# Two transformer layers on one core: closing steps cut into pieces among products, the token table turned later, opening loads reordered

## The chip, the core and the metric

The kernel runs on one core of a Trainium2 chip, all in fp32. The metric is the device time of one execution in microseconds. The core has a matrix engine (TensorE, PE in the profile), a vector engine (VectorE, DVE), an activation engine (ScalarE, ACT), a general engine (GpSimd, POOL) and a queue engine that issues transfers (SyncE, SP); ACT and POOL can issue transfers too. Each engine takes its instructions in order, and engines wait for each other by semaphores.

## The reference, cut to what matters

The input is x, 8 sequences of 256 tokens of width 512. Two layers follow each other; each normalizes x and adds an attention part and a feed-forward part to it.

```python
# layer 0, attention: 32 heads of 128, with decays along the sequence
qkv = silu(xn @ qkv_w.T)
attn = blockwise(q, k, v, decays)            # (q k^T * decay) v, causal
xf = attn * rsqrt(mean(attn * attn over all 4096) + EPS)
a0 = (sigmoid(xn @ gate_w.T) * norm_w * xf) @ out_w.T
# layer 0, feed-forward: 16 experts, 2 chosen per token, and a shared one
scores = softmax(xn @ router_w + router_b) + router_bias   # best 2 of 4 groups, best 2 in them
y = sum over chosen e: score[e] * ((silu(xn @ w1[e] + b1[e]) * (xn @ w2[e] + b2[e])) @ w3[e] + b3[e])
x = x + a0 + y + shared(xn)
# layer 1, attention: one head of 128, softmax; feed-forward: 64 pieces of rank 16
G = softmax of the 16 best of xn @ Wr.T, zero elsewhere    # [tokens, 64]
f1 = (h * G) @ B * 2.0, with h = xn @ A.T
x = x + softmax_attention(xn) + f1
```

## The kernel before

**Staging.** The 2048 tokens are four chunks `i` of 512 (four tiles `t` of 128). The opening (to about 148 us) normalizes the chunks, routes the tokens, runs the shared expert (L355) and transposes the rows; PE is warmed by `WARM` transposes of the identity (L205). Then come 32 units `(i, g)`, one for each chunk and each of eight groups of four heads, chunk by chunk. A unit's projections q, k, gate, v are made by products of quarters of tokens and weights in the manner of Strassen: seven named products p1 to p7 in the order of `ORDER`, each by an inner scheme of seven more (`go`, L724); in chunk 0 some are plain and use eight. Weights' sums are made in chunk 0 (`w<-w,st` with `st` a staged part of the weights, `w<-w`) and stored for later chunks.

**Slots and pieces.** After each inner product the code calls `slot()`; a unit has 49 slots of about 1.47 us and lasts 72 to 77 us. `later(after, f)` puts the piece `f` on a list, to be run at the slot `now + after` or a later one: a slot runs one piece (two if more than 12 wait), and pieces whose names are on a list count for nothing. Through pieces run the quarter's silu and gate, scores (L846, L847) and attention (L858, L859), the projections through out_w (L935, L955, `acc<-ps_sc,acc`), experts and scatters.

**Experts.** The tokens of one expert tile (47 tiles) are fetched by an expert object: two gathers on POOL's queue (L761 rows, L766 weights), then `turn` transposes them (L775, copied to `xeT` by DVE in L777), `bias` gathers a bias on POOL (L781), `up` multiplies by w1, w2 (L793) and `down` by w3 (L805), after which DVE adds the bias to `ye` and SP stores it. A unit from number 8 on runs two or three experts, 16 slots apart.

**Table.** In chunk 0 `scatter` writes token numbers into a table in DRAM by indirect DMA on POOL; in unit 7 `read_table` loads it into `rows` (47 rows of 8 KB, SP's queue), and `turn_table` 16 slots later copies it to `byno` (DVE), transposes that on PE and copies it to `whose` (DVE), from which experts gather.

**Chunk's end.** `done()` is run about 22 slots into the unit behind a chunk's last one. It sums squares on PE (L1024, eight products of two tiles each), takes the root mean (`rms`), `combine`s the seven parts of `acc` on POOL (chunks 1 and 2 only), `finish`es into `r`, a staged `spare` (DVE, L636), and stores that to `xs_`.

**Second layer.** For each chunk: two `low_rank` calls (`seven`, L1573, with `hg` = product times `spread_g`, gates spread over ranks), then a third `seven` for the second matrix (L1651). A `fill` gives functions to run between the seven products (keys are the product just made): attention of layer 1, and in the third call the next chunk's head (route, q and k, values, softmax, gates). `gather` on POOL fetches the experts' results, `settle` adds them (DVE, L611), `normalize` prepares the next chunk (`spare<-x,mv,rstd`, L256), and `turn_rows` transposes it (L276).

**Order.** PE, DVE and SP are ordered by a planner from the program's order, save for instructions in `tc.keep_in_program_order`. In layer 0, ACT and POOL keep the order of the program.

Of the kernel before, what the change touches and what calls it, by code (L numbers as in the profile page):

```python
# [10 lines left out]
WARM = 16  # L11
SAME = 16
# [57 lines left out]
def block_kernel(  # L70
# [80 lines left out]
    scratch = big("scratch").rearrange("p (h b) n -> p h (b n)", h=4)  # L151
    xs = [work.tile([P, TPC, C], FP, tag="x", name=f"x{i}", bufs=NCH) for i in range(NCH)]
# [3 lines left out]

    rw = once([P, NC, E], "rw")
    nc.sync.dma_start(out=rw, in_=router_w)
    rb = once([P, 1, E], "rb")
# [3 lines left out]
    wsh = staged("wsh")[:, 0 : NC * 2 * SH * P].rearrange("p (c n) -> p c n", c=NC)  # L163
# [3 lines left out]
    bsh_t = once([P, 2, SH], "bsh_t")  # L167
    nc.sync.dma_start(out=bsh_t, in_=b_sh)
    for i in range(1, NCH):
        for t in range(TPC):  # L170
            nc.sync.dma_start(out=xs[i][:, t, :], in_=x_t[i, t])
# [27 lines left out]
    nc.scalar.dma_start(out=wsh, in_=w_sh)  # L199
# [183 lines left out]
    xT, gates, xns = [], [], []  # L383
# [68 lines left out]
    def begin(i):  # L452
        xns.append(work.tile([P, TPC, C], FP, tag="xn", name=f"xn{i}"))
        normalize(xns[i], xs[i], apart=(i == 0), behind=(i == 1))
# [3 lines left out]
    def turn(i):  # L458
        xT.append(work.tile([P, NC, CH], FP, tag="xT", name=f"xT{i}", bufs=3))
        for t in range(TPC):  # L460
            turn_rows(xT[i], xns[i], t, ps_mm())
# [144 lines left out]
    def settle(i, n, x_, y):  # L606

        for t in range(TPC):
# [13 lines left out]
    def combine(i):  # L622

        for o, p in (
            ("p2", "p1"), ("p6", "p1"), ("p7", "p6"), ("p6", "p5"), ("p3", "p6"), ("p4", "p7"), ("p5", "p7"),
        ):
# [3 lines left out]
    def finish(i, r):  # L630

        for b in range(2):
            for t in range(2):
                n = 2 * b + t
                o = r[:, n, :].rearrange("p (h c) -> p h c", h=2)
                nc.vector.scalar_tensor_tensor(  # L636
                    o, acc[i][:, 2 * b : 2 * b + 2, t], all_rms[i][:, n : n + 1], o, ALU.mult, ALU.add
                )

# [9 lines left out]
    with tc.tile_pool(name="attn", bufs=1) as attn, tc.manual_schedule(engines={mybir.EngineType.Activation, mybir.EngineType.Pool}):  # L649
# [94 lines left out]
        def slot():  # L744
# [3 lines left out]
            while pieces and pieces[0][0] <= now[0] and n < (2 if len(pieces) > 12 else 1):  # L748
                f = pieces.pop(0)[2]
                f()  # L750
                n += getattr(f, "func", f).__name__ not in ("silu", "bias", "gate", "read_table", "scatter", "load_sum", "sums1", "sums2", "sums3", "sums4", "settle0", "settle1", "out_sum")
# [135 lines left out]
        class Unit:  # L887
# [129 lines left out]
            def done(self):  # L1017
# [4 lines left out]
                for t in range(TPC):  # L1022
                    for n in range(2):
                        mm(  # L1024
# [736 lines left out]
```

## Time and profile before

| | us |
|---|---|
| median of 3 runs | 2821.71 (2817.76 to 2827.4) |
| profiled execution | 2825.62 |
| its span | 2823.9 |
| PE busy | 2753.2 (97%) |
| DVE, POOL, ACT busy | 1626.7 (58%), 1642.1 (58%), 950.7 (34%) |
| mean granted PE clock | 0.993 |

In what follows a timeline row is: start, length, engine, line, operation, out<-in with sizes, count, and in brackets the idle time ahead of it on its engine with what ended it. A row of waits is: engine and what waited, what it waited for, us in all, times, longest. "Granted clock" is the share of full speed at which PE was allowed to run.

### The profile page before, as it was taken

To read this page: it belongs to the slowest core of one execution; us is meant where nothing else is said; L and a number is where in the kernel's file an instruction comes from. 1 tells how busy PE (TensorE), PEld (TensorE's weight loads), DVE (VectorE), ACT (ScalarE), POOL (GpSimd) and SP (SyncE) were. 2 spreads that over 40 slices of the span, in tenths; PEclk is the share of its full clock that TensorE was granted. 3 is DMA by queue.
4 is the path that set the end of the run, shared out by engine and by line. 5 is a ranking of instruction groups with operands and counts; after the bars stand their busy time and mean duration, and the time that the engine had idled before them with its cause. 6 is when DMAs were issued, how large, how long until landed. Compare 5 with 4: busy or idle time off the path is not lost.

```text
span 2823.9 us, 49588 instructions
## 1 busy us (share of the span) xinstructions
PE 2753.2 (97%) x19641; PEld 2541.2 (90%) x19641; DVE 1626.7 (58%) x2722; ACT 950.7 (34%) x1685; POOL 1642.1 (58%) x1414
## 2 busy tenths in 40 slices
PE   9999999998999999999999999999999999999999
PEld 5699999997999999999899999999999999987877
DVE  7666677776445555555545555555455555656663
ACT  5232222221343333333343333333433333431211
POOL 6477777765556666666655555557555567642220
PEclk9999999999999999999999999999999999999999
DMA  7898888887877777777877777787877788652211
GB/s 288 323 336 328 325 332 332 314 310 300 323 296 292 276 285 271 284 265 294 303 255 269 261 262 272 272 300 279 295 260 263 276 308 311 220 221 68 77 55 62
DMA packets 155063, 752.67 MB, mean 267 GB/s; under 512 B 18721, under 2 KB 25249, under 8 KB 103457
## 3 DMA queue, kind: packets, MB, share of 16 engines
q1 hardware_dynamic: 136528, 677.62, 64.4%
q0 software_dynamic: 17872, 70.32, 7.5%
q8 instruction: 155, 2.54, 0.3%
q10 hardware_dynamic: 432, 1.57, 0.1%
q14 instruction: 76, 0.62, 0.1%
HBM read 605.66 MB, written 142.99 MB: 265 GB/s over the span
## 4 chain that ended last, share of the span: by engine, by line
PE 80%; DVE 7%; DMA 5%; issue 4%; POOL 3%; ACT 0%; SPq 0%; DVEq 0%; POOLq 0%; ACTq 0%
PE ps_a L724 23%; PE ps_e L724 12%; PE ps_sc L935 9%; PE ps_b L724 6%; PE ps_o L858 3%; PE ps_sc L846 3%; PE ps_sc L955 3%; PE ps_sc L793 3%; PE ps_o L859 2%; PE ps_a L1651 2%; PE ps_sc L847 2%; DVE w L100 1%; PE ps_a L1573 1%; PE ps_sc L805 1%; DVE r L100 1%
## 5 line engine op out<-in xcount | busy, mean ns | idle before, releaser
L724 PE MATMUL ps_a<-xt,w 128*128 128x128 f32 x5376 | 751.0, 276 | 13.3 <-DVE r L100 7.1
L724 PEld LDWEIGHTS ps_a<-xt,w 128*128 128x128 f32 x5376 | 685.8, 192 | 39.2 <-issue 12.2
L100 POOL TENSOR_TENSOR c<-c 128x512 f32<-128x512 f32 x240 | 302.7, 1276 | 251.1 <-DVE c L100 242.7
L100 POOL TENSOR_TENSOR c<-c,r 128x512 f32<-128x512 f32 x264 | 347.0, 1335 | 173.1 <-DVE r L100 171.6
L1077 ACT COPY cp<-ps_a 128x512 f32<-128x512 f32 x384 | 224.1, 584 | 607.7 <-PE ps_a L724 586.5
L724 PE MATMUL ps_e<-xt,w 128*128 128x128 f32 x2688 | 375.7, 276 | 8.1 <-DVE c L100 6.7
L724 PEld LDWEIGHTS ps_e<-xt,w 128*128 128x128 f32 x2688 | 342.4, 193 | 16.7 <-DVE c L100 7.3
L100 POOL TENSOR_TENSOR w<-w 128x512 f32<-128x512 f32 x224 | 297.4, 1335 | 100.8 <-DVE w L100 39.7
L724 PE MATMUL ps_a<-w,xt 128*128 128x128 f32 x1792 | 346.4, 275 | 0.0
L100 POOL TENSOR_TENSOR sums<-sums,sq 128x512 f32<-128x512 f32 x120 | 155.7, 1298 | 291.5 <-ACT sq L873 283.7
L935 PE MATMUL ps_sc<-wo,gT 128*128 128x256 f32 x1288 | 305.0, 380 | 1.1 <-POOL gT L100 1.1
L724 PEld LDWEIGHTS ps_a<-w,xt 128*128 128x128 f32 x1792 | 272.0, 192 | 0.0
L935 PEld LDWEIGHTS ps_sc<-wo,gT 128*128 128x128 f32 x1288 | 232.7, 191 | 26.0 <-POOL gT L100 1.3
L100 DVE TENSOR_TENSOR acc<-ps_sc,acc 128x512 f32<-128x512 f32 x208 | 142.6, 690 | 189.6 <-PE ps_sc L935 149.8
L100 DVE TENSOR_TENSOR c<-ps_a,c 128x512 f32<-128x512 f32 x216 | 146.9, 688 | 140.7 <-PE ps_a L724 135.6
L878 DVE SCALAR_TENSOR_TENSOR gT<-ps_o,nw,c 128x256 f32<-128x256 f32 x256 | 112.0, 479 | 190.5 <-ACT sq L873 182.2
L724 PE MATMUL ps_b<-xt,w 128*128 128x128 f32 x1536 | 214.1, 276 | 7.0 <-issue 5.5
L724 PEld LDWEIGHTS ps_b<-xt,w 128*128 128x128 f32 x1536 | 195.0, 192 | 14.8 <-issue 11.0
L821 ACT ACTIVATE c<-c 128x512 f32<-128x512 f32 x256 | 150.1, 629 | 156.2 <-DVE c L100 138.1
L873 ACT ACTIVATE sq<-ps_o 128x512 f32<-128x512 f32 x120 | 71.7, 597 | 372.4 <-PE ps_o L859 367.5
L100 DVE TENSOR_TENSOR s<-ps_sc,decay 128x384 f32<-128x384 f32 x256 | 140.0, 552 | 69.9 <-PE ps_sc L847 67.5
L724 PE MATMUL ps_e<-w,xt 128*128 128x128 f32 x896 | 173.9, 276 | 0.0
(306 smaller groups left out, 4754.4 us busy)
## 6 DMA issues: line engine op xcount, KB each, us to landing
w<-in_w_att_dram SPq DMA_DIRECT2D x128, 1024.0 KB
st<-in_w_att_dram SPq DMA_DIRECT2D x32, 1024.0 KB
wo<-in_w_out_dram SPq DMA_DIRECT2D x113, 256.0 KB
decay<-dec SPq DMA_DIRECT2D x64, 384.0 KB
w<-ws0p SPq DMA_DIRECT2D x12, 1792.0 KB
w<-ws1p SPq DMA_DIRECT2D x12, 1792.0 KB
w<-ws2p SPq DMA_DIRECT2D x12, 1792.0 KB
w<-ws3p SPq DMA_DIRECT2D x12, 1792.0 KB
```

The lines of the kernel that those rows point to most:

```text
L100: (eng or nc.vector).tensor_tensor(o, a, b, op)
L724: mm(bank[:, bass.ts(ty, P)], a, b, start=(first and ty == 0), stop=True, skip_group_check=True,)
L793: mm(pu[:, bass.ts(n, P)], w12[:, n, c, :], self.xeT[:, c, :], start=(c == 0), stop=(c == NC - 1),)
L821: nc.scalar.activation(qk, qk, AF.Silu)
L846: mm(p[:, 0:S], self.c[:, 2 * hh, P : 2 * P], q, start=True, stop=True)
L847: mm(p[:, S : S + P], self.c[:, 2 * hh + 1, P : 2 * P], q[:, 1, :], start=True, stop=True,)
L858: mm(po[:, bass.ts(hh, S)], v[:, 0, :], self.s[:, hh, 0:S], start=True, stop=False)
L873: nc.scalar.activation(sq, po, AF.Square)
L878: nc.vector.scalar_tensor_tensor(gT[:, h, :].rearrange("p (t n) -> p t n", t=2), po[:, bass.ts(h, S)].rearrange("p (t n) -> p t n", t=2), ...
L935: mm(py[:, bass.ts(t, S)], self.O[p][:, hh, bass.ts(t, P)], self.wo[p][:, hh, :], start=(t == 0 and hh == 0), stop=(hh == 1), skip_group_c ...
L955: mm(py[:, bass.ts(h, S)], gT[:, hh, bass.ts(t, P)], self.wo[pair, h][:, hh, :], start=(h == 0 and hh == 0), stop=(hh == 1), skip_group_ch ...
L1077: nc.scalar.copy(c, bank)
```

## The change

- Opening: `WARM` is 28 instead of 16; the load of `wsh` is the third on SP's queue instead of on ACT's; `bsh_t` comes behind `rw`; x of chunks 1 to 3 comes ahead of `w3sh`. `xT0` and `xn0` are allocated at the top (not shown below).
- Scatters come about 30 slots later in chunk 0, spread over units 0 to 6.
- `turn_table` runs at slot 36 behind the read instead of 16, its first copy pinned.
- `done()` takes squares of two tiles, then one slot later the other two and the root; the seven combining steps are a piece each, one to a slot; the finishing of each tile is a pinned piece; the store is a piece.
- Experts: `up` at 14 instead of 13, `down` at 19 instead of 18; in units that begin a chunk the first expert is at slot 24 (before: 1 in unit 8, 20 in units 16 and 24) and there are two; unit 15 has three.
- Second layer: `gates` and the spreading run as a fill behind the product p1 (`filled(1)` is new); settling, statistics, scaling and the last chunk's finishing are split over fills and pinned, where they ran between the calls.

```diff
@@ -8,7 +8,7 @@
 FP = mybir.dt.float32
-WARM = 16
+WARM = 28
 SAME = 16
@@ -149,26 +149,29 @@
     scratch = big("scratch").rearrange("p (h b) n -> p h (b n)", h=4)
+    xT = [work.tile([P, NC, CH], FP, tag="xT", name="xT0", bufs=3)]
+    xns = [work.tile([P, TPC, C], FP, tag="xn", name="xn0")]
     xs = [work.tile([P, TPC, C], FP, tag="x", name=f"x{i}", bufs=NCH) for i in range(NCH)]
...
+    wsh = staged("wsh")[:, 0 : NC * 2 * SH * P].rearrange("p (c n) -> p c n", c=NC)
+    nc.sync.dma_start(out=wsh, in_=w_sh)
     rw = once([P, NC, E], "rw")
     nc.sync.dma_start(out=rw, in_=router_w)
+    bsh_t = once([P, 2, SH], "bsh_t")
+    nc.sync.dma_start(out=bsh_t, in_=b_sh)
     rb = once([P, 1, E], "rb")
...
     nc.sync.dma_start(out=rbias, in_=router_bias.to_broadcast([P, E]))
-    wsh = staged("wsh")[:, 0 : NC * 2 * SH * P].rearrange("p (c n) -> p c n", c=NC)
+    for i in range(1, NCH):
+        for t in range(TPC):
+            nc.sync.dma_start(out=xs[i][:, t, :], in_=x_t[i, t])
     held = staged("held")
...
     nc.sync.dma_start(out=w3sh, in_=w3_sh)
-    bsh_t = once([P, 2, SH], "bsh_t")
-    nc.sync.dma_start(out=bsh_t, in_=b_sh)
-    for i in range(1, NCH):
-        for t in range(TPC):
-            nc.sync.dma_start(out=xs[i][:, t, :], in_=x_t[i, t])
     nw = const.tile([P, H], FP, name="nw")
@@ -196,7 +199,6 @@
     nc.scalar.activation(root[:, 0:1], eps_t, AF.Sqrt)
-    nc.scalar.dma_start(out=wsh, in_=w_sh)
     ident = const.tile([P, P], FP, name="ident")
@@ -603,9 +607,9 @@
-    def settle(i, n, x_, y):
-        for t in range(TPC):
+    def settle(i, n, x_, y, ts=range(TPC)):
+        for t in ts:
             gate = slot_gates[:, n, i * TPC + t : i * TPC + t + 1]
@@ -619,23 +623,26 @@
-    def combine(i):
-        for o, p in (
-            ("p2", "p1"), ("p6", "p1"), ("p7", "p6"), ("p6", "p5"), ("p3", "p6"), ("p4", "p7"), ("p5", "p7"),
-        ):
+    COMBINED = (
+        ("p2", "p1"), ("p6", "p1"), ("p7", "p6"), ("p6", "p5"), ("p3", "p6"), ("p4", "p7"), ("p5", "p7")
+    )
+    def combine(i, steps=COMBINED):
+        for o, p in steps:
             o, p = (acc[i][:, SEVEN.index(n)] for n in (o, p))
...
-    def finish(i, r):
-        for b in range(2):
-            for t in range(2):
-                n = 2 * b + t
-                o = r[:, n, :].rearrange("p (h c) -> p h c", h=2)
+    def finish(i, r, ns=range(TPC), kept=lambda ins: ins):
+        for n in ns:
+            o = r[:, n, :].rearrange("p (h c) -> p h c", h=2)
+            at = 2 * (n // 2)
+            kept(
                 nc.vector.scalar_tensor_tensor(
-                    o, acc[i][:, 2 * b : 2 * b + 2, t], all_rms[i][:, n : n + 1], o, ALU.mult, ALU.add
+                    o, acc[i][:, at : at + 2, n % 2], all_rms[i][:, n : n + 1], o, ALU.mult, ALU.add
                 )
+            )
@@ -748,7 +755,7 @@
                 f()
-                n += getattr(f, "func", f).__name__ not in ("silu", "bias", "gate", "read_table", "scatter", "load_sum", "sums1", "sums2", "sums3", "sums4", "settle0", "settle1", "out_sum")
+                n += getattr(f, "func", f).__name__ not in ("silu", "bias", "gate", "read_table", "scatter", "load_sum", "sums1", "sums2", "sums3", "sums4", "settle0", "settle1", "out_sum", "combine", "finish", "store")
@@ -1019,21 +1026,36 @@
                 pr = ps_sc()
-                for t in range(TPC):
-                    for n in range(2):
-                        mm(
-                            pr[:, t : t + 1],
-                            sums_[i][:, t // 2, n * S + t % 2 * P : n * S + (t % 2 + 1) * P], ones,
-                            start=(n == 0), stop=(n == 1),
-                        )
-                rms = small.tile([P, TPC], FP, tag="rms", name="rms", bufs=NCH)
-                rsqrt(rms, pr[:, 0:TPC], 1.0 / (H * HD))
-                all_rms[i] = rms
+                def squares(ts):
+                    for t in ts:
+                        for n in range(2):
+                            mm(
+                                pr[:, t : t + 1],
+                                sums_[i][:, t // 2, n * S + t % 2 * P : n * S + (t % 2 + 1) * P], ones,
+                                start=(n == 0), stop=(n == 1),
+                            )
+                def means():
+                    squares((2, 3))
+                    rms = small.tile([P, TPC], FP, tag="rms", name="rms", bufs=NCH)
+                    rsqrt(rms, pr[:, 0:TPC], 1.0 / (H * HD))
+                    all_rms[i] = rms
+                def store():
+                    nc.sync.dma_start(out=xs_[i], in_=self.r)
+                squares((0, 1))
+                later(1, means)
+                after = 2
                 if 0 < i < NCH - 1:
-                    combine(i)
+                    for n in range(7):
+                        later(after + n, partial(combine, i, COMBINED[n : n + 1]))
+                    after += 8
                 if i + 1 < NCH:
-                    finish(i, self.r)
-                    nc.sync.dma_start(out=xs_[i], in_=self.r)
+                    for n in range(TPC):
+                        later(after + 1 + n, partial(finish, i, self.r, (n,), tc.keep_in_program_order))
+                    later(after + 1 + TPC, store)
@@ -1147,7 +1169,7 @@
         FROM = NG
-        EARLY = 7
+        EARLY = 8
         todo = list(range(NMT))
@@ -1162,8 +1184,8 @@
             later(12, e.bias)
-            later(13, e.up)
-            later(18, e.down)
+            later(14, e.up)
+            later(19, e.down)
@@ -1182,14 +1204,16 @@
             def turn_table():
-                nc.vector.tensor_copy(
-                    byno[0:NMT], rows.bitcast(I32).rearrange("j (p o) -> j p o", o=SAME)[:, :, 0]
+                tc.keep_in_program_order(
+                    nc.vector.tensor_copy(
+                        byno[0:NMT], rows.bitcast(I32).rearrange("j (p o) -> j p o", o=SAME)[:, :, 0]
+                    )
                 )
...
-            later(16, turn_table)
+            later(36, turn_table)
@@ -1293,12 +1317,12 @@
                 if i * NG + g >= FROM:
-                    for e in range(3 if i * NG + g < FROM + EARLY else 2):
+                    for e in range(3 if g > 0 and i * NG + g < FROM + EARLY else 2):
                         if todo:
-                            later((20 if g == 0 and i > 1 else 1) + 16 * e, partial(expert, todo.pop(0)))
+                            later((24 if g == 0 else 1) + 16 * e, partial(expert, todo.pop(0)))
                 if i == 0:
-                    for e in range(5 * g, min(5 * g + 5, TOP * NTT)):
-                        later(5 + 10 * (e - 5 * g), partial(scatter, e // TOP, e % TOP))
+                    for e in range(max(5 * g - 3, 0), 5 * g + 2 if g < NG - 1 else 0):
+                        later(10 * (e - 5 * g) + 35, partial(scatter, e // TOP, e % TOP))
                     if g == NG - 1:
@@ -1352,6 +1376,7 @@
         c1 = copied(a)
+        filled(1)
         b = ps_b()
@@ -1412,7 +1437,6 @@
             last_bias(x_, work.tile([P, C], FP, tag="sb3", name="sb3", bufs=1))
-            finish(i, x_)
         return x_
@@ -1537,7 +1561,6 @@
     head.softmax()
-    head.gates()
     for i in range(NCH):
@@ -1565,7 +1588,12 @@
-            gates2 = [spread(h * HJ + j) for h in range(2)]
+            gates2 = []
+            def spread_both():
+                gates2.extend(spread(h * HJ + j) for h in range(2))
+            fill = {1: [*fill.get(1, ()), spread_both], **{k: f for k, f in fill.items() if k != 1}}
@@ -1623,13 +1651,35 @@
                 gather(i + 1, n, following[1 + n])
-        low_rank(0, {2: [partial(turned, 0)], 7: [partial(turned, 1)], 5: [partial(weighed, 0)], 3: [partial(weighed, 1)]})
-        for n, y in enumerate(following[1:]):
-            settle(i + 1, n, following[0], y)
-        low_rank(2, {k: [partial(attended, t)] for t, k in enumerate((2, 7, 5, 3))})
+        fill1 = {
+            1: [head.gates] if i == 0 else [],
+            2: [partial(turned, 0)], 7: [partial(turned, 1)], 5: [partial(weighed, 0)], 3: [partial(weighed, 1)], 4: [],
+        }
+        fill2 = {k: [partial(attended, t)] for t, k in enumerate((2, 7, 5, 3))}
+        fill2[4] = []
         if following:
             settled[i + 1] = spare()
-            normalize(settled[i + 1], following[0])
+            whole = Normal(settled[i + 1], following[0])
+            def stats(t):
+                whole.stats(t, tc.keep_in_program_order)
+            def scaled(t):
+                tc.keep_in_program_order(whole.scaled(t))
+            if i + 2 == NCH:
+                for k, ns in ((2, (0, 1)), (7, (2, 3))):
+                    fill1[k].append(partial(finish, i + 1, following[0], ns, tc.keep_in_program_order))
+            for n, fill, k, ts in (
+                (0, fill1, 5, (0, 1)), (0, fill1, 3, (2, 3)), (1, fill1, 4, (0, 1)), (1, fill2, 2, (2, 3)),
+            ):
+                fill[k].append(partial(settle, i + 1, n, following[0], following[1 + n], ts))
+            fill2[7] += [partial(stats, 0), partial(stats, 1)]
+            fill2[5] += [partial(stats, 2), partial(stats, 3), whole.root]
+            fill2[3] += [partial(scaled, 0), partial(scaled, 1)]
+            fill2[4] += [partial(scaled, 2), partial(scaled, 3)]
+        low_rank(0, fill1)
+        low_rank(2, fill2)
         if i + 1 < NCH:
...
                 yT1 = xT[0]
```

## The prediction

> **What bounds the kernel now.** I read the page's head and its chain first, then TensorE's waits, then stretches of the timeline around each wait.
>
> ```profile
> span 2823.9 us, 49588 instructions
> PE 2753.2 (97%) x19641; PEld 2541.2 (90%) x19641; DVE 1626.7 (58%) x2722; ACT 950.7 (34%) x1685; POOL 1642.1 (58%) x1414
> PE 80%; DVE 7%; DMA 5%; issue 4%; POOL 3%; ACT 0%; SPq 0%; DVEq 0%; POOLq 0%; ACTq 0%
> ```
>
> TensorE (PE) is the bound. The change leaves its products as they are (12 tiny warm-up transposes more), so it can win only in PE's 2823.9 - 2753.2 = 70.7 us of idle time, and in the half clock that follows some of it. The waits of PE (reason, total us, times, longest) say where that is:
>
> ```profile
> PE ps_sc L955 <- DVE gT L878: 8.8, 1, 8.8
> PE ps_sc L793 <- DVE xeT L777: 7.7, 6, 1.3
> PE ps_a L724 <- DVE r L100: 7.1, 16, 1.1
> PE ps_e L724 <- DVE c L100: 6.7, 3, 4.4
> PE ps_e L1573 <- DVE cp L100: 4.0, 2, 3.7
> PE ps_sc L276 <- DVE spare L256: 3.0, 3, 2.2
> PE ps_b L276 <- DVE xn L256: 2.8, 1, 2.8
> PE ps_sc L1530 <- DVE v L100: 2.2, 1, 2.2
> PE ps_sc L1024 <- DVE ye L100: 2.1, 1, 2.1
> ```
>
> All but the third and the eighth are touched by the change. The third is the ordinary product's, about 0.4 us in each unit.
>
> **The clock, a first rule to weigh.** Busy time by stretches shows a granted clock of 0.57 over 753 to 757 us, 0.58 over 1381 to 1385, 0.53 over 2573 to 2576.5 and 0.57 over 2702 to 2706, each just behind one of the longer waits; the records give 0.5 for one piece of 3.413 us, so one such dip costs 3.41 / 2 = 1.7 us. It followed waits of 2.1 us and more, and none of 1.8 or less. The Trainium skill ("TensorE: Matmul & The Clock Gate", Part 1: The HAM clock gate, and its oscillation section) has the drop after an idle window and asks for no gaps over about 3.4 us. By that rule the waits of 2.1 to 2.8 us cost themselves alone, and curing unit 8, the opening and the second layer's 2.17 us wait would save about 5 us less. I go by the row.
>
> **Part by part.**
>
> *Opening.*
>
> ```profile
> 8.23 0.66 PE L276 MATMUL ps_b<-ident,xn 128*128 128x128 f32 x4 [2.78 <-DVE xn L256]
> 11.04 5.14 PE L311 MATMUL ps_sc<-rw,xT 128*128 128x16 f32 x24
> 16.02 4.21 PE L355 MATMUL ps_b<-xT,wsh 128*128 128x512 f32 x5
> ```
>
> The warm-up of 16 transposes ends at 5.45; xn is there at 8.23; the clock is 0.5 from 9.449 to 19.689 (three pieces). Twelve more transposes, at the 0.213 us pitch until 6.0 and half of that after, end near 7.0, so the wait is 1.2 us instead of 2.78 and the piece at 9.449 should stay at full clock. The 24 passes of scores then take about 2.9 us instead of 5.1, and the shared expert starts near 13.7 instead of 16.02: 2.3 us. It would win 1.8 more at full clock over its first 3.7 us; but the scores' 16-column products may look idle themselves, as they seem to near 36.8 us where another dip stands, which takes that back. wsh goes from ACT's queue (issued 4.82, landed 13.28) to SP's third place, ahead of router and biases; it must not hold the last of x's first rows (landed 6.04), which it may for a microsecond. Ends 0 and 4.1; I take 2.8. Everything to 120 us is bound by PE, so it reaches the end. Twelve later x loads move ahead of w3sh, which the shared expert needs only after its first products.
>
> *Table.* The scatters on POOL come 30 slots later (0.14 us iota and 1.0 us indirect DMA each, on POOL at 58%), the last still about 20 us ahead of the read: nothing. What the read does:
>
> ```profile
> 666.43 0.26 DVE L1185 CAST byno<-rows 47x128 f32<-47x128 int32 x1 [13.34 <-DMA rows<-table]
> ...
> 671.46 2.50 DVE L100 TENSOR_TENSOR w<-w,st 128x512 f32<-128x512 f32 x4 [1.59 <-DMA st<-in_w_att_dram]
> ```
>
> rows is issued at 645.31 and lands 21.10 us later. DVE stands 13.34 us in front of byno, the gate products queued behind it come late, and PE loses 8.82 us plus one dip, 10.5 in all. At slot 36, pinned, byno waits for nothing: by that row, 10.5 us go. A second rule speaks against it. "DMA: Bandwidth & Descriptors" (Why a DMA increments its semaphore by 16 and not by 1) says that a copy runs on the largest number of engines up to 16 that divides its slowest dimension; 47 rows are prime, so one engine carries it all, and a later transfer's share on that engine comes behind. The trace agrees, and shows the cost: of w, issued at 645.73, the landings are in by 651.41 but one, at 668.88; of st, issued at 651.33, by 656.67 but one, at 671.36. The change leaves the read as it is. So DVE stands next at the second row, w<-w,st, until about 671.4; the first p5 product of PE needs the third of these four, ready near 673.2, against 675.57 before. PE, with 5.4 us of work at full clock from 659.5 and some 0.7 to 1.3 of L846/L847 moved ahead of it, arrives near 665.7, loses 7.5 us there, and pays a dip of 1.7 to 3.3 behind it. 2.4 + 1.0 - 2.5 is 0.9; I take 1, between -1 and 3.
>
> *First chunk's end (unit 8).* The squares L1024 stood behind an expert's down product: DVE's ye waited 7.50 us for a bias gather, PE 2.14, and a dip followed. An expert issues three gathers of 1.0 to 1.3 us on POOL and a store on SP. They now begin at slot 24, behind the squares, so this pair is not there: 3.8; one set goes to unit 15, where units 9 to 14 already carry as many. With two experts instead of three a 1.10 us wait at 782 may go too: 0 to 4.9, taken 3.8.
>
> *Combining (units 16 and 24).*
>
> ```profile
> 1368.93 9.41 POOL L100 TENSOR_TENSOR acc<-acc 128x512 f32<-128x512 f32 x7
> ...
> 1375.49 4.73 DVE L636 SCALAR_TENSOR_TENSOR spare<-acc,rms,spare 128x512 f32<-128x512 f32 x4 [3.61 <-POOL acc L100]
> ...
> 1381.34 1.43 PE L724 MATMUL ps_e<-xt,w 128*128 128x128 f32 x6 [4.37 <-DVE c L100]
> ```
>
> POOL does seven additions in a run, DVE waits for them 3.61 us in finish, the `s` and `c` that PE needs are behind it, and PE stands 4.37, then dips: 6.1. In unit 24 it is 1.71 and no dip. One step to a slot of about 1.47 us adds 1.34 of POOL work per slot for seven slots; POOL falls up to some 5 us behind its usual work, which feeds the gates, so not all goes: of 7.8, I take 6.2, between 2 and 7.8. The finishes are pinned on DVE after POOL's last step with 4 slots between, 0.6 to 0.8 each, so they should wait for nothing; if they did, the `c` adds behind them would be late as before. The store leaves SP's queue about slot 37, ahead of the w and wo loads, which SP takes in order.
>
> *Experts.*
>
> ```profile
> 863.48 0.68 DVE L777 COPY xeT<-ps_sc 128x512 f32<-128x512 f32 x1
> ...
> 864.21 2.05 PE L793 MATMUL ps_sc<-xeT,xw 128*128 128x128 f32 x16 [1.28 <-DVE xeT L777]
> ```
>
> xeT is ready at 864.16; PE is there at 862.93. One slot later it first does a product and one L846/L847 pair, 1.55 us, and reaches L793 at 864.48, 0.3 behind xeT. The rest of the pair's inputs are there: their `c` was activated earlier, and the third bank of ps_sc is free. So six waits of 1.28, one in each of units 9 to 14, go: 7.7. The margin is thin; I take 7.3, between 4 and 7.9. L805 moves as far as L793, so its distance stays.
>
> *Second layer.* PE's order hardly moves (12 + 4 transposes become 8 + 8). The 2.21 us wait at 2533 stays: the gates still need G. At 2569.38 PE waits 2.17 for the scaled rows and dips. DVE is full from 2551.2 to 2570; one settle (0.67) moves into its idle time ahead of that, and two scaled go ahead of the last hg (0.6), so the first eight transposes start 1.3 earlier and the dip goes: 2.4 of 3.9, less what the second eight lose. At 2697.57 PE waits 3.74 for cp, behind four finishes (5.74 us, themselves on POOL's bias adds); two of them now come behind it, but an hg does not, so 0.6 and half a dip: 1.4. Together 3.5 after 0.3 for the split; ends 0 and 8.
>
> *Sum.* 2.8 + 1 + 3.8 + 6.2 + 7.3 + 3.5 = 24.6, less 2 for small new waits (an estimate: four or five of the 0.3 to 0.6 kind that the waits show) = 22.6. The profiled execution took 2825.62, its span and 1.7 outside; the sum makes it 2803.0. It lies 3.9 above the runs' median of 2821.71, so 2799.1 there. All low ends make 5 less, all high ones 43.
>
> **Rivals.**
> - *The table's stall goes whole*: PE's p5 product doesn't find st late, or catches up later. For it: byno is the wait that the chain names. Against: the landing of st at 671.36. 9.5 us more: 2790.
> - *Half is eaten*: DVE and POOL, each 58% busy, are late for the next thing wherever PE no longer waits (the margin of 0.3 at the experts, POOL's lag in unit 16). 6 to 12 us remain: 2812.
> - *Slower*: the second expert's gather (slot 40) takes the buffer that the stored sum leaves, so on POOL's in-order queue it waits for the store's landing, three slots (4.4 us) after its issue. Behind it stand POOL's `c` adds, which ACT and then PE wait for. The store took 3.8 us in this trace (1380.28 to 1384.12), so the wait is short. POOL can be about 2 us late unseen; beyond that each microsecond counts at each of three chunk ends, with 1.7 for the dip. To eat 22.6 and 8.5 more, each would have to lose 10.4, 8.7 of it waiting: the store would have to land 15 us after its issue. Only what stood behind the table read took so long. It decides from there: 2832.
>
> **How the numbers follow.** Likeliest 0.58 (2793 to 2809), table 0.16, half eaten 0.2, slower 0.06. A measurement here can tell 0.3%, 8.5 us. A third of the half-eaten case lies within that, with the likeliest's tail 0.09 the same. Range 2784 (table, and high ends) to 2815 (half eaten).
>
> **What would show it.** Right: no L793 <- xeT; byno unwaited but w<-w,st still waiting for st until about 671, with PE's ps_b wait of 6 to 8 us there; POOL's acc adds single; no dip at the units' turns; PE near 13.7 at wsh. Wrong: a wait of POOL's gather on a store, a new PE wait above 2 us in units 8, 16 or 24, or x's landing past 7 us.

## The result: 0.35% faster, less than half of what was forecast

The changed kernel takes 2812.75 us (median of 20 runs, 2808.36 to 2819.32), the kernel before 2823.99 (20 runs, 2817.76 to 2831.43). The ratio is 0.9965, with a 95% interval of 0.9957 to 0.9972: 8 to 12 us faster. The forecast was 22.6 us faster. The profiled execution took 2814.99 us with a span of 2813.1, against 2825.62 and 2823.9.

The page's head and TensorE's waits (what waited, for what, us in all, times, longest) of the changed kernel; L731 is the products' line (L724 before), L1601 that of the second layer's products:

```profile
span 2813.1 us, 49529 instructions
...
PE 2752.4 (98%) x19653; PEld 2538.8 (90%) x19653; DVE 1630.7 (58%) x2722; ACT 947.6 (34%) x1683; POOL 1645.8 (59%) x1414
```

```profile
PE ps_a L731 <- DVE r L100: 7.8, 16, 1.1
PE ps_b L731 <- DVE w L100: 6.2, 1, 6.2
...
PE ps_a L731 <- ACT cp L1099: 5.2, 3, 1.8
PE ps_sc L278 <- DVE spare L258: 4.1, 4, 2.2
PE ps_e L1601 <- DVE cp L100: 3.8, 1, 3.8
...
PE ps_sc L942 <- POOL gT L100: 2.4, 2, 1.2
PE ps_sc L1554 <- DVE v L100: 2.2, 1, 2.2
...
PE ps_e L731 <- DMA w<-ws5p: 1.3, 1, 1.3
```

The six waits for xeT, the wait for gT behind byno, the squares' wait for ye and the 4.4 us wait of unit 16 are gone. New are a wait of 6.2 us for `w` in unit 7 and two of 1.67 us for `cp` copied by ACT, in units 16 and 24. PE's idle time fell from 70.7 to 60.7 us.

The products are the same 12800 instructions in almost the same order in both kernels, so the difference of the start times of the first, second and so on says where time was won between the two profiled executions (minus is earlier in the changed kernel):

| place (by the kernel before) | from, to | won or lost there |
|---|---|---|
| opening and first products, to 190 us | 0, +1.8 | +1.8 |
| to 583 | +1.8, +0.1 | -1.7 |
| to 642 | +0.1, +0.6 | +0.5 |
| the table's stall, to 680 | +0.6, -0.7 | -1.3 |
| to 729 | -0.7, -0.4 | +0.4 |
| units 8 to 16, to 1465 | -0.4, -10.8 | -10.5 |
| unit 24, to 2054 | -10.8, -9.9 | +0.9 |
| to 2452 | -9.9, -9.8 | +0.1 |
| second layer, to the end | -9.8, -10.8 | -1.0 |

### The profile page after: what moved, and what is told of

Same layout as the page of the kernel before. It is cut to its first block, busy times and chain, and to the rows that moved or that the text cites. A ratio compares the mean times of both kernels' runs of the same rounds, so it can differ in the third digit from the quotient of the medians.

```text
span 2813.1 us, 49529 instructions
## 1 busy us (share of the span) xinstructions
PE 2752.4 (98%) x19653; PEld 2538.8 (90%) x19653; DVE 1630.7 (58%) x2722; ACT 947.6 (34%) x1683; POOL 1645.8 (59%) x1414
## 4 chain that ended last, share of the span: by engine, by line
PE 85%; DVE 6%; DMA 4%; issue 2%; POOL 2%; ACT 1%; another core or an unknown queue 0%; SPq 0%; DVEq 0%; POOLq 0%; ACTq 0%
PE ps_a L731 25%; PE ps_e L731 12%; PE ps_sc L942 10%; PE ps_b L731 7%; PE ps_o L865 4%; PE ps_sc L962 3%; PE ps_sc L853 3%; PE ps_sc L800 3%; PE ps_a L1601 2%; PE ps_o L866 2%; PE ps_sc L854 2%; PE ps_a L1701 2%; DMA st<-in_w_att_dram 2%; DVE w L100 1%; PE ps_sc L812 1%
## 5 line engine op out<-in xcount | busy, mean ns | idle before, releaser
L731 PE MATMUL ps_a<-xt,w 128*128 128x128 f32 x5376 | 752.9, 276 | 17.2 <-DVE r L100 7.8
L731 PEld LDWEIGHTS ps_a<-xt,w 128*128 128x128 f32 x5376 | 687.8, 192 | 47.3 <-issue 14.1
L731 PE MATMUL ps_e<-xt,w 128*128 128x128 f32 x2688 | 374.8, 276 | 5.2 <-DVE c L100 1.6
L731 PEld LDWEIGHTS ps_e<-xt,w 128*128 128x128 f32 x2688 | 341.3, 192 | 12.1 <-issue 4.8
L731 PE MATMUL ps_a<-w,xt 128*128 128x128 f32 x1792 | 346.9, 275 | 0.0
L731 PEld LDWEIGHTS ps_a<-w,xt 128*128 128x128 f32 x1792 | 272.6, 192 | 0.0
L731 PE MATMUL ps_b<-xt,w 128*128 128x128 f32 x1536 | 216.0, 277 | 13.1 <-DVE w L100 6.2
L731 PEld LDWEIGHTS ps_b<-xt,w 128*128 128x128 f32 x1536 | 196.1, 194 | 16.0 <-issue 12.6
L731 PE MATMUL ps_e<-w,xt 128*128 128x128 f32 x896 | 173.5, 275 | 0.0
```

The source lines that it names most:

```text
L731: mm(bank[:, bass.ts(ty, P)], a, b, start=(first and ty == 0), stop=True, skip_group_check=True,)
```

## The experiments

Each was run beside the kernel before. A ratio without another word is to that kernel; the changed kernel's own is 0.9965.

### The changed kernel again: half clock is partly chance

No edit.

> The changed kernel once more, nothing edited. It should be 10 us under the kernel before (8 to 13). Theory on the clock: whether a wait of PE of 1.8 to 2.3 us is followed by a stretch of 3.41 us at half clock depends on where it lies in a free-running window of that length, so the stretches of half clock behind such waits (127.8 and 653.4 in the profile of the changed kernel, 2535 and 2573 in that of the kernel before) should not all be at the same waits in this profile; those behind waits over 3.4 us should be. Rival: they belong to the place in the program, and are the same again.

2813.99 us, 0.9961 (0.9947 to 0.9975). The waits came back, the half clock did not. PE's wait of 2.2 us for the gates G is in every profile of this study. In the kernel before it was followed by a stretch at half clock; in the first profile of the changed kernel it was not, and in this one it was. The stretches around it, before and then in the first profile of the changed kernel (stretch, its length, busy us and instructions of PE, PEld, DVE, ACT, POOL, granted clock, DMA share, GB/s):

```profile
2531.90:2535.31 3.41, 1.20 (x7) 0.72 (x6) 3.41 (x20) 0.70 (x2) 1.21 (x1) 1.00 1.05 416
2535.31:2538.72 3.41, 3.41 (x11) 2.64 (x12) 3.37 (x14) 1.62 (x7) 0.00 (x0) 0.50 0.72 293
```

```profile
2520.55:2523.96 3.41, 2.33 (x14) 1.77 (x12) 3.41 (x28) 0.90 (x3) 2.38 (x2) 1.00 1.03 400
2523.96:2527.38 3.42, 2.29 (x12) 1.81 (x13) 3.42 (x17) 0.79 (x3) 0.00 (x0) 1.00 0.99 404
2527.38:2530.79 3.41, 3.41 (x21) 2.82 (x20) 2.81 (x10) 2.43 (x10) 0.00 (x0) 1.00 0.23 76
```

In each of the 14 profiles of this study all changes of the granted clock lie on one grid with steps of 3.413 us, and these stretches are windows of that grid. Before, one window holds the whole wait (PE busy for 1.20 us of it), and the next is at half clock. In the changed kernel an edge of the grid splits the same wait (busy 2.33 and 2.29 us), and the clock stays full. This one wait was followed by half clock in 9 of the 14 profiles: in those nine, one window holds at least 2.05 us of idle time, in the other five 1.86 us at most.

The count over all profiles, between 300 and 2780 us, says the same. Of the windows at full clock, 52 of the 53 with 2.0 us or more of PE idle were followed by one at half clock, 9 of the 43 with 1.6 to 2.0 us, and 1 of the 9991 with less. A window already at half clock was followed by another in 21 of 21 cases with 0.6 us or more idle, in none of the 62 with less.

So the program sets the wait, and whether its dip of 1.7 us follows depends on where the edges of the grid fall, which differs between executions. The prediction weighed two rules: the dip always follows waits of 2.1 us and more (its one profile), or gaps matter only past some 3.4 us (the Trainium skill, "TensorE: Matmul & The Clock Gate", HAM oscillation). The runs lie between.

### Opening

`e_open_only` is the kernel before with the opening's edits alone, `e_open_old` the changed kernel without them.

```diff
-WARM = 16
+WARM = 28
+    nc.sync.dma_start(out=wsh, in_=w_sh)
...
-    nc.scalar.dma_start(out=wsh, in_=w_sh)
```

> The kernel before with the new opening alone (28 warm-up transposes, wsh third on SP's queue, x ahead of w3sh). Theory: the first transposes start 0.8 us earlier, but ACT has the decays' exponentials ahead of its copies of xT, the scores end 0.3 us later instead of 2.3 earlier, and the low clock lasts 2.3 us longer: 1 to 3 us slower than the kernel before, all of it there by 200 us. Rival, the prediction's step: 2.8 us faster. Rival, cut off by the stream of weights at about 570 us: no change at the end.

2825.34 us (14 runs), 1.0004 (0.9996 to 1.0012): between 1.1 us faster and 3.4 slower, which leaves out the 2.8 us gain of the prediction.

> The changed kernel with the opening of the kernel before: 16 warm-up transposes, wsh on ACT's queue, x behind w3sh. Theory: what the opening does to the time is cut off at about 575 us, where DVE waits for st in both profiles at the same microsecond (568.7 and 568.8) however late PE is. So by the first products PE is about 1.3 to 1.8 us earlier than in the changed kernel, a wait of 1.7 us comes back at about 574, and from 583 on nothing is left: within 1 us of the changed kernel. Rival: the opening is bound by PE to the end, as the prediction had it, and the old one ends 1.8 us earlier (since the new one was that much later at 190 us).

2809.24 us (6 runs), 0.9961 (0.9944 to 0.9979), too wide to tell from 0.9965. The profiles tell more. The 513th product starts at 202.2 to 202.8 us in the five profiles with the old opening and at 203.4 to 206.2 in the eight with the new one (means 202.5 and 204.4). At the 3073rd, near 650 us, the means are 650.2 and 653.9. So the new opening costs about 2 us, which on the mean is not made up by 650 us. The wait near 574 us, which the expectation counted on, did not come back in `e_open_old`. It comes and goes with the landing of st, in kernels with either opening. The 1.7 us won there in the first pair of profiles were chance. The scatters' new places, which no run has alone, don't show: from the 513th product to about 572 us the four profiles with the old ones take 368.6 to 369.6 us, the ten others 368.0 to 369.8.

Why the opening got worse is in the changed kernel's timeline (start, length, engine, line, operation, in brackets the idle time before it and what ended it):

```profile
7.39 0.65 PE L278 MATMUL ps_b<-ident,xn 128*128 128x128 f32 x4 [0.83 <-DVE xn L258]
...
10.64 1.76 ACT L403 ACTIVATE decay<-dist 128x384 f32<-128x384 f32 x4
...
12.31 1.05 ACT L281 COPY xT<-ps_a 128x512 f32<-128x512 f32 x2
...
12.92 3.59 PE L313 MATMUL ps_sc<-rw,xT 128*128 128x16 f32 x16 [1.10 <-ACT xT L281]
...
16.36 6.47 PE L357 MATMUL ps_b<-xT,wsh 128*128 128x512 f32 x8
```

The first transposes start 0.84 us earlier, as forecast. But DVE scales the first two rows before it has the statistics of the last, ACT's fourth root comes at 9.03 (before: by 7.9), its table load for the exponentials and four of these follow, and the copies of xT stand behind them until 12.31 (before 10.91). PE waits 1.10 us for these and starts the shared expert at 16.36. All eight profiles of this opening have that wait of 1.10 us and start it at 14.75 to 16.36.

The old opening's own start, 16.02, was a matter of the clock: of its five profiles that is the only one where all of the scores ran at half clock, and the other four start the shared expert at 14.12 to 14.31. So most of the 2.3 us that the prediction meant to win there was lost in that one execution only.

`e_open_dve` puts all four copies on DVE:

```diff
-        if t % 2:
+        if t % 2 and xn is not xns[0]:
             nc.scalar.copy(o, i)
```

> The changed kernel with all four copies of chunk 0's xT on DVE instead of two on ACT. Theory: the second half of the scores waits 1.10 us for ACT's copies, which stand behind four exponentials of 1.76 us; on DVE they are done at about 12.1 instead of 13.4, the wait goes and the shared expert starts about 1 us earlier, at 15.3 instead of 16.36; the low clock behind the scores stays[...]: 1 us less than the changed kernel (0 to 2.5). Rival: the clock stays up once there is no wait, and 3 to 4 us are won.

2811.35 us (4 runs), 0.9954 (0.9939 to 0.9968): not to be told from the changed kernel by its time. In its profile the wait is gone, the shared expert starts at 13.55 (the prediction's 13.7), and the 513th product starts at 201.2 us, 3.3 earlier than in the changed kernel's first profile and 0.9 earlier than in any old opening; by 650 us 1.2 of the 3.3 are left. One window of 3.4 us at half clock follows the scores, against three in the changed kernel's profile, so part of the 3.3 is the clock. It follows although PE had no gap; most of what it did were the short products of the scores (16 columns):

```profile
10.79:14.20 3.41, 3.41 (x28) 3.12 (x27) 3.41 (x9) 1.70 (x4) 1.45 (x2) 1.00 1.06 354
14.20:17.62 3.42, 3.42 (x6) 1.36 (x5) 3.42 (x11) 2.11 (x3) 1.09 (x1) 0.50 1.04 355
```

### The table's read

`e_split` is the changed kernel, and `e_split_before` the kernel before, with this edit:

```diff
-            nc.sync.dma_start(out=rows, in_=table.rearrange("(j p) o -> j (p o)", p=P).bitcast(FP))
+            listed = table.rearrange("(j p) o -> j (p o)", p=P).bitcast(FP)
+            nc.sync.dma_start(out=rows[0:32], in_=listed[0:32])
+            nc.sync.dma_start(out=rows[32:NMT], in_=listed[32:NMT])
```

In the changed kernel the turn waits for nothing, and DVE and PE wait for st instead:

```profile
671.85 2.50 DVE L100 TENSOR_TENSOR w<-w,st 128x512 f32<-128x512 f32 x4 [9.30 <-DMA st<-in_w_att_dram]
...
673.85 1.62 PE L731 MATMUL ps_b<-xt,w 128*128 128x128 f32 x6 [6.21 <-DVE w L100]
```

> The changed kernel with the read of the table as two transfers, of 32 and of 15 rows, instead of one of 47. Theory: the one transfer of 47 rows goes by one DMA engine for 20 us and holds back the last sixteenth of each transfer behind it; in two parts it lands within some 3 us, st at about 657 instead of 671.8, the 6.2 us wait of PE at the first p5 product of unit 7 goes with the half clock behind it (6.8 us at half, 3.4 lost), so about 8 us less than the changed kernel (6 to 10), 18 less than before. Rival: something else is late next there, POOL's sums of w, and 2 to 4 us are won. Rival: the table's rows are slow to read however they are split, and nothing changes.

2807.73 us (4 runs), 0.9941 (0.9924 to 0.9957): 6.3 less than the same kernel unsplit beside it. The same sums of DVE, with nothing to wait for:

```profile
663.36 2.49 DVE L100 TENSOR_TENSOR w<-w,st 128x512 f32<-128x512 f32 x4
```

> The kernel before with the table's read in two transfers of 32 and 15 rows, and the turn left 16 slots behind the read. Theory: the one engine that carried all 47 rows was the cause of the whole stall; with it gone byno waits for nothing at slot 16 already, and the later turn of the change is worth nothing by itself: 8 to 11 us less than the kernel before (the wait of 8.82 and about 1.7 for the half clock). Rival: the read takes long because it waits on the scatters or on DRAM, byno still waits, and only a few microseconds are won.

2814.77 us (15 runs), 0.9974 (0.9966 to 0.9982): 7.3 us less than before (5 to 10), a little less than the 8 to 11 expected, with the turn left at slot 16. In its profile the turn is reached at once:

```profile
656.47 0.25 DVE L1187 CAST byno<-rows 47x128 f32<-47x128 int32 x1
```

So this one edit wins three quarters of what the whole change wins. The landings show why. In the changed kernel the read of the table lands in one part at 666.79, and of `st`, issued at 652.14, fifteen parts are in by 657.83 and the last at 671.76. In `e_split_before` the two reads land in sixteen and in fifteen parts, all within 4.6 us of their issue, and all sixteen parts of `st`, issued at 649.00, are in by 653.73. The 47 rows by one DMA engine were the cause, as the Trainium skill has it in "DMA: Bandwidth & Descriptors" (Why a DMA increments its semaphore by 16 and not by 1): 32 and 15 rows can be shared by 16 and 15 engines.

### Experts one slot later

`e_experts` is the kernel before with this alone:

```diff
-            later(13, e.up)
-            later(18, e.down)
+            later(14, e.up)
+            later(19, e.down)
```

> The kernel before with the experts' up and down one slot later, and nothing else of the change. Theory: the six waits of 1.28 us for xeT go, 7.7 us, and a wait for w<-ws5p of about 1.3 with one of 0.3 takes their place, so 6 us faster than before (5 to 8). Rival, that DVE and POOL are late for the next thing anyway: 3 us or less.

2820.22 us (20 runs), 0.9992 (0.9984 to 0.9999): 2.3 us faster (0.3 to 4.5), less than the 6 expected. In the profile the six waits are gone and units 9 to 14 are 9.4 us shorter together. Unit 8 is 3.7 us longer:

```profile
758.91 1.02 POOL L761 DMA_INDIRECT xw<-xnd,whose  x1 [16.27 <-DVE c L100]
...
765.59 1.12 PE L775 MATMUL ps_sc<-ident,xw 128*128 128x128 f32 x4 [6.74 <-DMA xw<-xnd,whose]
```

SP issues the store of the finished sum at 753.26; the trace has its last landing at 758.13, and POOL issues the third expert's gather 0.78 us behind that. The gather takes the buffer that the stored sum leaves. (The profile names a sum of DVE that ended at 758.68; the distance of 0.78 us is that of `e_comb_dve` below, 0.76, where it names the store.) PE waits 6.74 us for the gathered rows and runs at half clock until 769.59, 4.0 us behind the wait. The change has later slots for experts in unit 8, so that this wait is not in its profile; the two parts belong together. The profiled execution, at 2814.24 us, is one of the two fastest of the 20. Unit 8 takes back less than half of what units 9 to 14 win in it, so why the median gained only 2.3 us is not shown.

### The chunk's end

In the changed kernel three rows of unit 16 carry its 1.67 us:

```profile
1382.97 0.59 ACT L950 COPY acc<-ps_sc 128x512 f32<-128x512 f32 x1 [9.23 <-DVE spare L642]
...
1384.10 0.94 PE L731 MATMUL ps_a<-xt,w 128*128 128x128 f32 x6 [1.67 <-ACT cp L1099]
...
1389.74 1.00 POOL L768 DMA_INDIRECT xw<-xnd,whose  x1 [5.99 <-DVE c L100]
```

`acc` has one buffer. ACT's first copy of the next chunk's acc waits 9.23 us for the last finish, now at 1382.87 (1380.2 before), and the copies of banks behind it on ACT's queue are late for PE. The row of POOL becomes important below: the finished sum's store landed at 1388.99, 0.75 us before that gather. `e_vec` moves ACT's copy:

```diff
                 if self.g == 0:
-                    nc.scalar.copy(o, py)
+                    nc.vector.tensor_copy(o, py)
```

> The changed kernel with the first copies of a chunk's acc (chunks 1 to 3) by DVE instead of ACT. Theory: acc has one buffer, ACT's first copy of the next chunk waits 9.2 us for the last finish and holds up the copies of banks behind it, which is the wait of 1.67 us of PE in units 16 and 24; with the copy on DVE, behind the finishes in the same queue, both go: 3 us less than the changed kernel (2 to 3.6). Rival: the copies make DVE late for its sums, and the time stays or gets up to 3 us longer.

2813.86 us (8 runs), 0.9965 (0.9954 to 0.9975): no change. The wait for cp went, and one of 1.48 us for `r` stood 10 us later. It looked as if POOL had too much to do, so `e_comb_dve` gave the combining to DVE:

```diff
-            add(o, o, p, nc.gpsimd)
+            if len(steps) == 1:
+                tc.keep_in_program_order(nc.vector.tensor_tensor(o, o, p, ALU.add))
+            else:
+                add(o, o, p, nc.gpsimd)
```

> The changed kernel with the seven combining steps of a chunk pinned on DVE instead of POOL, one to a slot as before. Theory: POOL is what is late in units 16 and 24 (its seven additions of 1.3 us come on top of work it does just in time, it was 3.1 us idle between two of them for a sum that DVE had not made, and it ended its last at 1377.7, 0.6 us before the burst had ended in the kernel before); on DVE they take 0.7 to 1.8 us each beside POOL, finish ends some microseconds earlier, ACT's copy of the next acc waits less and POOL is in time: both waits of 1.67 us of PE go, 3 us less than the changed kernel (2 to 4). Rival: DVE gets late for the gates instead and the time stays or rises by up to 3.

2815.99 us (14 runs), 0.9979 (0.9969 to 0.9989): nothing won over the changed kernel, and rather some 4 us lost (the two intervals just overlap). The theory falls. POOL has less to do and is late all the same:

```profile
1388.55 1.00 POOL L771 DMA_INDIRECT xw<-xnd,whose  x1 [9.70 <-DMA xs<-spare]
...
1390.86 4.94 POOL L100 TENSOR_TENSOR c<-c,r 128x512 f32<-128x512 f32 x4
...
1393.39 0.58 ACT L1131 COPY r<-ps_a 128x512 f32<-128x512 f32 x1 [5.80 <-POOL c L100]
```

POOL stands 9.70 us before the second expert's gather until the store `xs<-spare` has landed; the c sums behind it are late, ACT waits 5.80 us for one of them and PE 2.17 for ACT, in units 16 and 24 alike. The store was issued at 1379.34 and landed at 1387.79. So `e_vec_later` adds to `e_vec`:

```diff
-                            later((24 if g == 0 else 1) + 16 * e, partial(expert, todo.pop(0)))
+                            later((24 + 5 * e if g == 0 else 1) + 16 * e, partial(expert, todo.pop(0)))
```

> The changed kernel with two edits: the first copies of acc on DVE, as tried before, and in units that begin a chunk the second expert at slot 45 instead of 40. Theory: with the copies on DVE alone the wait of PE did not go but moved some 10 us on, to r<-ps_a behind POOL's c<-c,r, because POOL stood in front of the second expert's gather until the store of the finished sum had landed (POOL idle 9.7 us for xs<-spare in the kernel with the combining on DVE, 6 us before that gather in the changed kernel). Five slots later the buffer is free, POOL does its c sums in time, and both waits of PE in each of units 16 and 24 go: 3 us less than the changed kernel (2 to 4.5). Rival: POOL is late there for its amount of work, and nothing is won.

2811.67 us (4 runs), 0.9957 (0.9942 to 0.9971), which the time alone can't tell from the changed kernel. In its profile the waits of 1.67 and 1.48 us are gone in both units (0.6 us for `r` is left), POOL issues the gather without standing for it, and the products gain 2.4 us over the changed kernel in unit 16 and 2.6 in unit 24:

```profile
1396.78 1.29 POOL L768 DMA_INDIRECT xw<-xnd,whose  x1
```

The same profile lost 3.9 us by 650 us, where the edits don't reach, mostly near 580 us, so what is shown here is shown by the profile and not by the time.

### Second layer

`e_second_old` is the changed kernel with the second layer of before (`gates`, `settle`, `normalize` and `finish` between the calls).

> The changed kernel with the second layer of the kernel before (gates and spreading ahead of the first product, settling, normalizing and finishing in runs between the calls). Theory: the split only lets DVE have the scaled rows some 1.7 us earlier once a chunk has that as its longest wait, which is the first one; the other differences of the two profiles there are half clock behind waits of 2.2 us that lies by chance. So 1 to 2 us more than the changed kernel. Rival, the prediction's step: 3.5 us more.

2813.2 us (8 runs), 0.9962 (0.9948 to 0.9976), the same as the changed kernel, though the interval still allows the 3.5 us. In the changed kernel's first profile the wait that was to shrink stands:

```profile
2559.70 1.11 PE L278 MATMUL ps_sc<-ident,spare 128*128 128x128 f32 x8 [2.17 <-DVE spare L258]
```

DVE has the first scaled row 1.7 us sooner, counted from PE's products with G; but PE, at full clock this time, is there 1.7 us sooner too. The wait at the last chunk is 3.78 us instead of 3.74, since cp is still behind the fourth finish.

The other profiles show the split at work, and that it wins nothing. In the five with the new second layer where half clock followed the wait for G, PE comes later and does not wait for the first scaled row at all; in the four where the clock stayed full it waits 2.17 us. But from the first layer's last product to the end the nine profiles with the new second layer take 325.7 to 328.7 us (mean 327.0), the five with the old one 323.5 to 327.9 (mean 325.5). Where the new one loses again was not followed.

### Together

`e_best2`: the changed kernel with the old opening, the read in two parts, the copy on DVE and the second expert at slot 45.

> The changed kernel with the opening of the kernel before, the table's read in two transfers, the first copies of acc on DVE and the second expert at slot 45. By what each showed or should show: 2 to 3.5 for the opening, 6 to 8 for the table, 3 for the chunk ends, so 11 to 14 less than the changed kernel, 2799 to 2803; rival, that these overlap: 2805 or more.

2798.0 us (4 runs, 2794.91 to 2803.54), 0.9917 (0.9902 to 0.9933): faster than both kernels. By the ratios it is 13.5 us less than the changed kernel, within the 11 to 14 that the parts should give. Its head and first waits:

```profile
span 2793.1 us, 49506 instructions
...
PE 2745.4 (98%) x19641; PEld 2535.2 (91%) x19641; DVE 1642.7 (59%) x2743; ACT 939.2 (34%) x1664; POOL 1647.3 (59%) x1414
```

```profile
PE ps_a L727 <- DVE r L100: 7.4, 16, 1.1
PE ps_b L727 <- issue: 5.4, 3, 2.0
```

There is no wait for w in unit 7, and at the ends of chunks none for cp and 0.6 us for r. PE's idle time is 47.7 us.

## Why the prediction was too high

The column "found" is worked out from the first pair of profiles where nothing else is said.

| term | predicted | found |
|---|---|---|
| opening | 2.8 won | about 2 lost (13 profiles); alone 1.1 won to 3.4 lost |
| table | 1 won | 1.3 won |
| unit 8 | 3.8 won | 1.3 won |
| combining | 6.2 won | 2.6 won |
| experts | 7.3 won | 6.1 won; alone 2.3 won (0.3 to 4.5) |
| second layer | 3.5 won | 1.0 won in the pair; nothing over 14 profiles |

- **Opening: the sign was wrong.** The step followed PE and DVE only. The copies of xT are on ACT, behind exponentials that ACT gets to later in the new order. The shorter wait for xn was right (1.2 forecast, 0.83 found), but PE's next waits were not looked at, and the last of them is for ACT. And the 16.02 that it started from was itself late by the clock (14.12 to 14.31 in the other four). By the profiles this term is off by some 5 us, the largest share of the shortfall of 12.
- **Table: right, in size and mechanism.** DVE waited for st until 671.85 (forecast 671.4), PE 6.21 us (7.5), and the dip followed. `e_split_before` shows the cause.
- **Unit 8.** The squares' wait is gone as said. The 1.10 us wait for `r` that "may go too" stayed, at the same product. New are 0.44 us for `c`, 1.26 for `s` near 780 and 0.83 for `r` near 788. What brings these was not tried.
- **Combining: the path was wrong.** "They should wait for nothing; if they did, the `c` adds behind them would be late as before", the step said. Finish ended 2.7 us later than before, and what waited for it was ACT's copy into the single acc, which the step didn't name. In unit 16, 6.45 us of waits and half clock became 2.16; a new wait of 1.23 us early in unit 16, less 0.41 that went at the end of unit 15, and 0.9 more in unit 24 took 1.7 back. The 1.23 us are for gT behind a POOL addition that stood 11.82 us for the bias `sb` (8.82 before); its load is issued behind the store of the `ye` of unit 15's third expert, which is new. That this is the cause was not tried.
- **Experts: right in the mechanism.** Six waits went; two waits for w<-ws5p and w<-ws3p, 1.6 us in all, came.
- **Second layer: the saving doesn't reach the end.** DVE had the scaled rows sooner, as said; that PE would come sooner too was missed, and the dip counted there depends on the grid. At the last chunk cp stayed behind the fourth finish, where the step had put two finishes behind cp.
- **The slower rival was real and small.** Its store landed 6 to 8.5 us after its issue where 3.8 had been read (unit 8's store in that same trace took 4.9), and it cost some 0.8 us at a chunk end of the changed kernel (the 2.4 and 2.6 that `e_vec_later` won, less the 1.67 for cp), not 10. Alone, without the later slots, the experts' edit paid 6.74 us and a dip to it.
- **The rival "half is eaten"** named 2812 us, and 2812.75 came. Its reason, something else late wherever PE no longer waits, holds for combining and unit 8. The opening and the second layer, which make up much of the shortfall, are not in it, so the close number is partly luck.
- **A slip in the sum.** The high ends of the six parts add to 35.7 us; the 43 that was stated needs the table's whole 10.5. The low ends add to 5 only without the 2 us for new waits.

The kernel before lay 2.3 us above the median of the first three runs when 20 were taken, which is no error of the sum.

## What to carry to other kernels

When a wait is removed, follow what its waiter feeds through every engine's queue, ACT's too, to the next thing that is late: here the opening and the combining stopped at a copy on ACT, the combining and the experts alone at a gather on POOL, each behind something else. Before a wait for a transfer is moved out of sight, ask why the transfer takes so long: here its row count kept it on one DMA engine, and splitting it won more than hiding it. A store of a staged buffer and the next use of that buffer on an in-order queue belong at least the store's landing apart, up to 8.5 us here. A time read from a single profile can be a matter of the clock: the late start that the opening's gain was counted from came in one profile of five.

## What was not expected of the hardware

The same wait of PE of 2.2 us was followed by 3.41 us at half clock in 9 of 14 profiles and by full clock in 5. What told them apart was the idle time inside one window of a fixed grid of 3.413 us: from about 2.0 us on the next window was at half clock, and once there 0.6 us kept it there. These are counts of this kernel, and they have exceptions. A window with no gap, filled mostly with 16-column products, was followed by half clock too (`e_open_dve`), so idle time in the records is not all that counts. What else does was not followed.

Past 300 us, waits of 1.5 to 1.95 us had a stretch of half clock starting within 3.4 us of them in 11 of 49 cases. The time at half clock differs from 25.9 to 44.8 us between the 14 profiles, up to 9.5 us of PE work by this count (an estimate, since part of it is idle). The runs of the changed kernel differ as much (2808 to 2819).
